# Two pre-norm layers on one core: first output weights two heads later, buffers of their own for x, and other places for layer 1's scale chain and bias quarters

## The chip, the cores and the metric

One core of a Trainium2 chip runs the kernel. The metric is the device time of one execution in microseconds (us). The times below are the median of three runs and one profiled execution. PE is TensorE (matmuls; PEld its weight loads), DVE VectorE, ACT ScalarE, POOL GpSimd, SP the engine whose queue issues the DMAs.

## The reference

Input x has 4 batches of 512 tokens with 1024 features, all float32. Two layers follow each other, each an attention and a feed-forward part with a residual addition and a layer norm in front:

```
x = x + L0_attn(ln(x))     # softmax over the 4 batches at each position
x = x + L0_ffn(ln(x), ...) # x @ W_base.T + b + LoRA of the top 2 of 8 experts
x = x + L1_attn(ln(x), ...)# 32 heads, causal, rope, low-rank q and kv; out @ wo.T
x = x + L1_ffn(ln(x), ...)
```

```
def _L1_ffn_ref(x, W, b, A, B, router_W, router_b):
    q = x[:, Q_START:Q_END, :].mean(axis=1)          # Q_START = 179, Q_END = -1
    routing = softmax(q @ router_W.T + router_b)     # 8 experts, one set per batch
    base = x @ W.T + b
    t = einsum('bsd,erd->bser', x, A)                # rank 16
    return base + einsum('bser,eor,be->bso', t, B, routing) * 2
```

## The kernel before

Tokens are cut into 16 tiles of 128. A float32 product is made as three matmuls of rounded parts: each operand is split into a high part h (rounded by a copy on ACT) and a low part l (the difference), and `matmul3` (L143 to L145) adds h*l, l*h and h*h in PSUM. Where both operands allow it, pairs of tiles and halves of the features make a 2 x 2 block product with seven products instead of eight; `STEPS` lists the seven (b11, t1, t2, b22, t3, b21, t4), with the PSUM bank and the quarter of the result of each. The operands of the seven steps are blocks and sums of blocks: s1, s2, s4, s3 (L934 on DVE), each split into h (ACT, L942: `ah`, `cxh`) and l (POOL, L943: `al`, `cxl`).

**Attention of layer 1** (about 430 to 1500 us of the profile) works on 4 groups of 8 heads, each on 4 batches. A loop over all heads u interleaves by hand the scores of head u (`pss`, with the mask and the row extremum on DVE in L868 and the exponential on ACT in L871), the transposes and values of the head before, the context of the pair before that, and, as a filler, either the output projection of the block before (`project`) or, in the first batch of a group, `prepare_output`. The latter multiplies slices of wo and wv into the output weights of the group: `block` (L1016: four matmuls into the PSUM tile poa or pob, which are read out by ACT in L1025 and L1030), and further steps that form and split their sums. `per` says how many steps of the filler are taken at each of three places of a head; 22 are needed. For the first block `per` is (0, 1, 2). The slices come by `fetch_output` on SP (2 x 512 KB and 64 KB for each two blocks), the next ones when a second half block has been issued. In this stretch a scheduler orders each engine's instructions by expected times; `issue_after` ties an instruction behind another one in its engine's order.

**The passage.** The projection of the last block (L1307 to L1330) is written for itself, with T, V, A and G in program order from there to the end (`manual_schedule`); SP's queue alone is still ordered by the scheduler. `fetch_last(j)` loads four 128 x 512 quarters of x from the scratch copy x_d into tiles xs of the pool xsp (order (0,0), (1,1), (0,1), (1,0)); each of the seven steps adds a product on DVE (L1328), and a finished quarter is stored (L1330). After the first add come the five small instructions of `scales` (L1245 to L1252) for the layer norm's scale and offset, and the next operand (s, cxh, cxl). Then load the weights of the last part, the bias row broadcast to all partitions (bias1, 512 KB), and rwT, rb, t3, t4.

**Layer 1's feed-forward** (about 1540 to 1776 us) runs over q = 0 to 7, each a pair of tiles, with seven steps of two products (columns 0 to 575 and 576 to 1151 of A and W together, 288 wide). One product is 12 matmuls, 1.60 us. Beside them in each step: `pair_sums`, `operand` (splits the operand two steps ahead), the statistics of the next pair (bn_stats L1519, bn_aggr L1520 in steps 1 and 2), `root` (ACT, L1238, step 2), `scales` (step 3), `norm` (ACT, L1260, steps 3 and 4), `turn1` (transposes L1269, steps 4 and 5). The product's results are added to x in place (`product`, L1458; its first 128 columns of LoRA inputs to `inputs`, L1454 and L1456). The LoRA of pair q - 1 follows within q: `weighed` multiplies inputs by the routing weights (hw, L1419), transposes (L1423), splits (hwh on ACT L1426, hwl on DVE L1428), and `lora` multiplies by B (lo, L143 to L145) and adds (L1412). For odd q this is at steps 2 to 5, for even q at steps 0 to 2; the routing weights rw are made by `mixture` (L1378 to L1400) at the turn from even to odd q.

`biased(q, n)` (POOL, L1436) adds one quarter of the bias row to a quarter of a tile of x, 128 x 256, in place: n = 0 to 3 for the first tile, 4 to 7 for the second. Before, pair q has two quarters at each of steps 1 to 4; those of q = 0 are at steps 0 to 3 of q = 1. They are issued behind the step's `operand` and ahead of its products:

```
            if q and 1 <= step < 5:
                for n in (0, 1):
                    biased(q, 2 * step - 2 + n)
            if q == 1 and step < 4:
                for n in (0, 1):
                    biased(0, 2 * step + n)
            if q:
                product(q, step, 0, h, l)
```

Of the kernel before, what the change touches and what calls it, by code (L numbers as in the profile page):

```python
# [9 lines left out]
F32 = mybir.dt.float32  # L10
# [7 lines left out]
P = 128  # L18
# [28 lines left out]
def block_kernel(ctx: ExitStack, tc: tile.TileContext, a: dict, out: bass.AP):  # L47
# [753 lines left out]
    with ExitStack() as c2:  # L801
# [17 lines left out]

        turn_of = [None]  # L820

        turned_in = [rdp.tile([P, 32], F32, name=f"ri{k}") for k in range(2)]
        for t in turned_in:
            G.memset(t, 0.0)
# [22 lines left out]
        def scores(u):  # L847

            g, b, i_ = units[u]
            f, h, l = queries.pop(u)  # L850
            _, kT, kF, _ = batches[g, b]
            p = pp.tile([P, 1280], F32, name="p")
            mn = small.tile([P, TPB], F32, name="mn")
            if i_ % 2 == 0:
                sums_of[0] = small.tile([P, 2, TPB], F32, name="rs2")
            rs2 = sums_of[0]
            rs = rs2[:, i_ % 2, :]
            for i in range(TPB - 1, -1, -1):
                n = (i + 1) * P
                ps = pss.tile([P, S], F32, name="pss")  # L860
                if i == 0:
                    T.matmul(ps[:, 0:n], lhsT=f[:, 0:P], rhs=kF, start=True, stop=True)
                else:
                    at = slice((i - 1) * P, i * P)
                    matmul3(ps[:, 0:n], h[:, at], l[:, at], kT[:, 0, 0:n], kT[:, 1, 0:n],
                            start=True, stop=True)
                to = p[:, OF[i] : OF[i] + n]
                turn_of[0] = V.tensor_tensor_reduce(out=to, in0=ps[:, 0:n], in1=causal[:, S - n : S], scale=1.0,  # L868
                                                    scalar=-NEG, op0=ALU.add, op1=ALU.min,
                                                    accum_out=mn[:, i : i + 1])  # L870
                A.activation(to, to, AF.Exp, bias=mn[:, i : i + 1], scale=-1.0,  # L871
                             accum_out=rs[:, i : i + 1])
                if i > 0:
                    yield
            if i_ % 2:
                divisors(u, rs2)
            probs[u] = p
            yield
# [122 lines left out]
        def prepare_output(g, fetched):  # L1001
# [9 lines left out]
            def block(n, half, at):  # L1011
                nonlocal fetched
                wo, wv = fetched
                po[at] = pso.tile([P, 512], F32, name="po" + at)
                for k in range(2):
                    T.matmul(po[at][k * KVR : (k + 1) * KVR, :], lhsT=wv[:, k, :],  # L1016
                             rhs=wo[k][:, half * 512 : half * 512 + 512], start=True, stop=True)
                if half and n + 1 < len(prs):
                    fetched = fetch_output(g, prs[n + 1])

# [135 lines left out]
        for u in range(NU + 3):  # L1156


            B, i = divmod(u - 3, HG)
            g, b = divmod(B, NB)  # L1160
            if i == 0 and B > 0:
                filler = project(*divmod(B - 1, NB))
            per = ((4, 1, 0) if i % 2 else (1, 1, 0)) if b else (2, 2, 2) if i >= HG // 2 else (3, 3, 1)
            if B == 0:
                per = (0, 1, 2)
            if b == 0 and i == (HG // 2 if g else 0) and g < NG:
                filler = prepare_output(g, wo_raw)
            sc = scores(u) if u < NU else iter(())
            tn = turn(u - 1) if 0 < u <= NU else iter(())
            if u >= 3 and u % 2:  # L1170
                cx = context(u - 3)
            advance(sc)
            advance(sc)
            advance(cx)
            advance(filler, per[0])
            if u + 1 < NU:
                split_query(u + 1)
            advance(sc)
            advance(sc)
            advance(tn)  # L1180
            advance(tn)
            advance(filler, per[1])
            if u < NU:
                g, b, i = units[u]
                if (b, i) == (NB - 1, 3) and g + 1 < NG:
                    wqs[2 * g + 2] = prepare_query(wq_raw, pso, "pob")
                if (b, i) == (0, 0) and g > 0:
                    wqs[2 * g + 1] = prepare_query(wq_raw, pso, "pob")
            if u + 2 < NU:
                query(u + 2, psq, "psq")  # L1190
            if u + 2 < NU:
                rotate_query(u + 2)
            advance(filler, per[2])
            advance(tn)
            if u < NU:
                g, b, i = units[u]
                if i == 2 and u + HG < NU:
                    nx = units[u + HG]
                    batches[nx[:2]] = load_batch(*nx[:2])
                if b == 0 and i == 0:  # L1200
                    wo_raw = fetch_output(g, 0)
                if (b, i) in ((NB - 1, 0), (NB - 1, 4)) and g + 1 < NG:
                    wq_raw = fetch_query(2 * g + 2 + i // 4)
                if (g, b) == (NG - 1, NB - 1) and i == 1:
                    late = raw()
                    hs = {0: [late[:, (t + 1) * D : (t + 2) * D] for t in range(2)]}
                    load_x(0, hs[0])
                    nc.sync.dma_start(out=late[:, 0:D], in_=a["b1T"])
                if (g, b) == (NG - 1, NB - 1) and i in (4, 5):
                    load_w1("t" + "12"[i - 4], 0, (0, 2)[i - 4])  # L1210
# [8 lines left out]
        w1p += [dp.enter_context(tc.tile_pool(name="d_w0", bufs=1))]  # L1219
        abp = dp.enter_context(tc.tile_pool(name="d_a", bufs=1))  # L1220
        splits = dp.enter_context(tc.tile_pool(name="d_split", bufs=3))
        ptp = dp.enter_context(tc.tile_pool(name="d_pt", bufs=2, space=PSUM))
        NP = NT // 2
        blocks, sums, roots, offs = {}, {}, {}, {}
# [78 lines left out]
        def fetch_last(j):  # L1303
            for t, k in ((0, 0), (1, 1), (0, 1), (1, 0)):
                at[j + t, k] = x_d[(NB - 1) * TPB + j + t][k]
                xs[j + t, k] = xsp.tile([P, 512], F32, name="xs")
                nc.sync.dma_start(out=xs[j + t, k], in_=at[j + t, k])  # L1307

        fetch_last(0)
# [4 lines left out]
        for n in range(14):  # L1314
# [36 lines left out]
                pair_sums(n - 10)  # L1351
            if n in (11, 12):
                parts.append(next(ops))
    w1p += [dp.enter_context(tc.tile_pool(name="d_w1", bufs=1, side="right"))]
    hp = dp.enter_context(tc.tile_pool(name="d_h", bufs=1))
    w1r = dp.enter_context(tc.tile_pool(name="d_c", bufs=1, side="right"))
# [5 lines left out]
        load_w1(kind, 1)  # L1362
    load_w1("t2", 1)
    fetch_h(1)
    bias1 = broadcast_rows(w1r, a["b1"], D, "bias1")
    rwT = w1r.tile([P, E, ND], F32, name="rwT")
    nc.sync.dma_start(out=rwT, in_=a["rwT"])
    rb = broadcast_rows(w1r, a["rb"], E, "rb")
    for kind in ("t3", "t4"):
        load_w1(kind, 1)  # L1370
    ones = w1r.tile([P, P], F32, name="ones")
    V.memset(ones, 1.0)
    bt1 = [w1r.tile([P, D], FR, name=f"b1{k}") for k in "hl"]
# [102 lines left out]
            split_w1("b22", 1, (step - 5,), V)  # L1476
    mix, at_work = None, {}

    def go_on(*keys):
        for k in keys:  # L1480
            next(at_work[k])

    for q in range(NP):
# [4 lines left out]
        for step in range(7):  # L1488

            if step == 6 and more:  # L1490
                pair_sums(0)
            if q and step < 2:
                for k in ((1, 2), (3,))[step]:
                    pair_sums(k)
# [5 lines left out]
            if odd and step in (1, 2):  # L1500
                rw[q // 2] = next(mix)
            if odd and step == 2:
                for t in range(2):
                    at_work[q - 1, t] = weighed(q - 1, t)
                    go_on((q - 1, t))
            if behind and step == 0:
                for t in range(2):
                    at_work[q - 1, t] = weighed(q - 1, t)
                    go_on((q - 1, t))
# [3 lines left out]
            if more and q + 1 >= TPB // 2:  # L1513
                if step == 1:
                    mv = small.tile([P, 2, 2], F32, name="mvd")
                if step in (1, 2):
                    st = small.tile([P, 2, 6], F32, name="st")
                    for c in range(2):
                        V.bn_stats(st[:, c, :], hs[q + 1][step - 1][:, c * 512 : (c + 1) * 512])  # L1519
                    V.bn_aggr(mv[:, step - 1, :], st)  # L1520
                if step == 2:
                    mv, r = root(mv, 2)
                if step == 3:
                    scales(mv, r, 2, range(2 * q + 2, 2 * q + 4))
            if more and step in (3, 4):
                norm(q + 1, step - 3)
            if q and 1 <= step < 5:
                for n in (0, 1):
                    biased(q, 2 * step - 2 + n)
            if q == 1 and step < 4:  # L1530
                for n in (0, 1):
                    biased(0, 2 * step + n)
            if q:
                product(q, step, 0, h, l)

            if (odd and step == 4) or (behind and step == 1):
                go_on((q - 1, 0), (q - 1, 1))
# [117 lines left out]
```

## Time and profile before

| | |
|---|---|
| runs of the kernel | 1781.0, 1783.48, 1784.86 us; median 1783.48 us |
| profiled execution | 1777.1 us, of which span 1775.3 us; around it 1.8 us |
| mean granted TensorE clock | 0.995 |
| ACT: exponentials of the scores (L871) | 512 x 559 ns = 284.5 us |
| POOL: splits `cxl` and others of 128 x 256 (L943) | 128 x 765 ns = 96.9 us |
| POOL: bias quarters (L1436) | 64, median 0.735 us each |
| DMA | 228.16 MB, mean 129 GB/s |

Times within the profile are microseconds from the span's start. The profiled execution stands at 6.4 us below the median of the runs, so differences are formed against its own time and then put on the median. In the timeline a row has start, length, engine, line, operation, what it writes and reads, and in brackets how long the engine had idled and what ended it. Matmuls are pipelined: rows of PE overlap.

### The profile page before, as it was taken

How to read it: one execution, taken by the hardware profiler on the slowest of the kernel's cores; microseconds unless marked ns; L12 is line 12 of the kernel's file. 1: busy time of each engine (PE TensorE's matmuls, PEld its weight loads, DVE VectorE, ACT ScalarE, POOL GpSimd, SP SyncE). 2: the span in 40 equal slices, each digit the busy share in tenths (PEclk: the TensorE clock that was granted, in tenths of full speed). 3: DMA queues.
4: the chain of work that ended last, by engine and by line, in shares of the span. 5: the costliest groups of instructions: out<-in, count | busy, mean ns of one | idle time of the engine just before them, and what ended most of it. 6: DMA issues, size and time to landing. Idle time of an engine off the chain costs nothing.

```text
span 1775.3 us, 31519 instructions
## 1 busy us (share of the span) xinstructions
PE 1724.4 (97%) x10536; PEld 1437.0 (81%) x10536; DVE 1315.3 (74%) x3516; ACT 904.0 (51%) x2319; POOL 884.3 (50%) x851
## 2 busy tenths in 40 slices
PE   6989999999999999999999999999999999999999
PEld 5989999998667778757777767778776877789998
DVE  6977885676787777687777787677778777587685
ACT  7422331365665555475555475555566555453332
POOL 0543441201556565546566545666555655575454
PEclk9999999999999999999999999999999999999999
DMA  4312454245133334352343353242354323944431
GB/s 191 120 51 92 165 172 130 84 137 184 57 123 129 98 106 136 108 180 87 120 132 101 115 188 108 93 148 93 127 164 135 118 100 114 328 159 136 140 111 61
DMA packets 131939, 228.16 MB, mean 129 GB/s; under 512 B 22272, under 2 KB 58752, under 8 KB 128448
## 3 DMA queue, kind: packets, MB, share of 16 engines
q1 hardware_dynamic: 131776, 226.13, 38.4%
q8 instruction: 84, 1.38, 0.3%
q14 instruction: 79, 0.65, 0.1%
HBM read 156.60 MB, written 71.83 MB: 129 GB/s over the span
## 4 chain that ended last, share of the span: by engine, by line
PE 85%; DVE 7%; DMA 3%; ACT 2%; issue 1%; POOL 1%; SPq 0%; DVEq 0%; POOLq 0%; ACTq 0%
PE psv L908 9%; PE pst L892 7%; PE pss L143 4%; PE pss L144 4%; PE pss L145 4%; PE po L143 4%; PE po L145 3%; PE po L144 3%; PE poa L143 3%; PE pob L143 3%; PE psq L143 3%; PE psq L145 3%; PE psq L144 3%; PE poa L144 3%; PE poa L145 3%; PE pob L145 3%
## 5 line engine op out<-in xcount | busy, mean ns | idle before, releaser
L871 ACT ACTIVATE p<-p,mn 128x512 f32<-128x512 f32 (+3 forms) x512 | 284.5, 559 | 206.0 <-DVE mn L868 205.8
L691 POOL TENSOR_TENSOR qf<-qf,ropeT 64x512 f32<-64x512 f32 x128 | 165.3, 1291 | 276.4 <-ACT qf L687 275.3
L868 DVE CUSTOM_DVE_ANT_0 p<-pss,causal 128x512 f32<-128x512 f32 (+3 forms) x512 | 231.2, 486 | 32.8 <-PE pss L145 25.5
L692 POOL TENSOR_TENSOR qf<-qf,t 64x512 f32<-64x512 f32 x128 | 165.7, 1294 | 41.0 <-DVE t L690 32.7
L892 PE MATMUL pst<-ident,p 128*128 128x128 f32 x1280 | 185.3, 273 | 0.7 <-ACT pT L894 0.7
L892 PEld LDWEIGHTS pst<-ident,p 128*128 128x128 f32 x1280 | 152.9, 141 | 25.6 <-ACT pT L894 2.4
L894 ACT COPY pT<-pst 128x512 f32<-128x512 f32 x256 | 141.7, 580 | 47.5 <-PE pst L892 46.7
L700 POOL TENSOR_TENSOR ql<-qf,qh 128x384 fp32r<-128x384 f32 x128 | 129.7, 1013 | 66.7 <-DVE qh L699 66.7
L143 PE MATMUL pss<-kT,ql 128*128 128x512 f32 (+2 forms) x384 | 144.6, 377 | 4.1 <-POOL ql L700 1.5
L943 POOL TENSOR_TENSOR cxl<-s,cxh 128x256 fp32r<-128x256 f32 x128 | 96.9, 765 | 89.5 <-ACT cxh L942 61.2
L143 PE MATMUL po<-w_h,hTl 128*128 128x384 f32 (+1 forms) x384 | 134.2, 350 | 0.6 <-DVE x L394 0.6
L145 PE MATMUL po<-w_h,hTh 128*128 128x384 f32 (+1 forms) x384 | 131.0, 341 | 0.0
L144 PE MATMUL pss<-kT,qh 128*128 128x512 f32 (+2 forms) x384 | 130.8, 341 | 0.0
L144 PE MATMUL po<-w_l,hTh 128*128 128x384 f32 (+1 forms) x384 | 130.7, 340 | 0.0
L145 PE MATMUL pss<-kT,qh 128*128 128x512 f32 (+2 forms) x384 | 130.3, 339 | 0.0
L894 DVE COPY pT<-pst 128x256 f32<-128x256 f32 x128 | 54.0, 422 | 96.3 <-PE pst L892 95.9
L687 ACT COPY qf<-psq 128x512 f32<-128x512 f32 x126 | 73.9, 587 | 70.3 <-PE psq L145 69.7
L689 DVE TENSOR_TENSOR t<-psq,ropeT 32x512 f32<-32x512 f32 x126 | 87.7, 696 | 23.9 <-ACT qf L687 19.9
L143 PEld LDWEIGHTS pss<-kT,ql 128*128 128x128 f32 x384 | 72.6, 189 | 39.3 <-POOL ql L700 11.2
L871 ACT ACTIVATION_READ_ACCUMULATOR p<-p,mn 128x1 f32 x512 | 97.4, 190 | 0.0
L690 DVE TENSOR_TENSOR t<-psq,ropeT 32x512 f32<-32x512 f32 x126 | 87.1, 691 | 1.8
L985 DVE TENSOR_TENSOR xs<-xs,pob 128x512 f32<-128x512 f32 x105 | 71.2, 678 | 19.6 <-PE pob L145 19.5
(563 smaller groups left out, 4977.6 us busy)
## 6 DMA issues: line engine op xcount, KB each, us to landing
xs<-x_d SPq DMA_DIRECT2D x128, 256.0 KB
x_d<-xs SPq DMA_DIRECT2D x128, 256.0 KB
slotC<-in_woT_dram SPq DMA_DIRECT2D x32, 512.0 KB
rb<-r_d SPq DMA_DIRECT2D x128, 128.0 KB
w_t<-raw SPq DMA_DIRECT2D x32, 288.0 KB
x<-in_x_dram SPq DMA_DIRECT2D x16, 512.0 KB
x_d<-x SPq DMA_DIRECT2D x32, 256.0 KB
slotA<-q_d SPq DMA_DIRECT2D x8, 1024.0 KB
```

The costliest lines, as they stand in the source:

```text
L143: T.matmul(ps, lhsT=al, rhs=bh, start=start, stop=False, **kw)
L144: T.matmul(ps, lhsT=ah, rhs=bl, start=False, stop=False, **kw)
L145: T.matmul(ps, lhsT=ah, rhs=bh, start=False, stop=stop, **kw)
L691: G.tensor_tensor(f[mid], f[mid], ropeT[mid, 0, :], ALU.mult)
L692: G.tensor_tensor(f[mid], f[mid], t2[mid], ALU.add)
L700: G.tensor_tensor(l, f[:, P:S], f32(h), ALU.subtract)
L868: turn_of[0] = V.tensor_tensor_reduce(out=to, in0=ps[:, 0:n], in1=causal[:, S - n : S], scale=1.0, scalar=-NEG, op0=ALU.add, op1=ALU.min, ...
L871: A.activation(to, to, AF.Exp, bias=mn[:, i : i + 1], scale=-1.0, accum_out=rs[:, i : i + 1])
L892: T.transpose(ps[:, w : w + P], p[:, OF[i] + j * P : OF[i] + (j + 1) * P], ident)
L894: copy(pT[:, AT[js[0]] : AT[js[0]] + w], ps[:, 0:w])
L908: T.matmul(ps[n * KVR : (n + 1) * KVR, S - w : S], lhsT=k[:, j, :], rhs=pTs[u + n][:, AT[j] : AT[j] + w], start=(j == 0), stop=(j == TPB - 1))
L943: G.tensor_tensor(l, src, f32(h), ALU.subtract)
```

## The change

Six edits, line numbers of the kernel before:

1. `prepare_output`'s blocks are tied behind the last score matmul that has been issued (`scored[0]`), and `per` of the first block becomes (0, 0, 0) for its first two heads and (0, 2, 2) from the third on.
2. A pool d_xl of three buffers takes the quarters (0,0), (1,1) and (0,1) that `fetch_last(0)` loads; (1,0) and the four of `fetch_last(2)` stay in xsp. The pool is closed after the projection.
3. The load of bias1 is issued behind those of t3 and t4.
4. `scales` moves from the head of step 3 to step 2, behind that step's first product.
5. For even q the two hw of `weighed` go ahead of `pair_sums` in step 0.
6. The bias quarters move: q = 0 to steps 0, 1 and 3 of q = 1 (three, three and two), even q to steps 3 to 6, odd q to steps 4 to 6 and step 0 of q + 1, q = 7 to steps 1, 3, 4 and 5.

```diff
                 if i == 0:
-                    T.matmul(ps[:, 0:n], lhsT=f[:, 0:P], rhs=kF, start=True, stop=True)
+                    scored[0] = T.matmul(ps[:, 0:n], lhsT=f[:, 0:P], rhs=kF, start=True, stop=True)
...
-                for k in range(2):
-                    T.matmul(po[at][k * KVR : (k + 1) * KVR, :], lhsT=wv[:, k, :],
-                             rhs=wo[k][:, half * 512 : half * 512 + 512], start=True, stop=True)
+                with tc.issue_after(scored[0].ins):
+                    for k in range(2):
+                        T.matmul(po[at][k * KVR : (k + 1) * KVR, :], lhsT=wv[:, k, :],
+                                 rhs=wo[k][:, half * 512 : half * 512 + 512], start=True, stop=True)
...
             if B == 0:
-                per = (0, 1, 2)
+                per = (0, 2, 2) if i > 1 else (0, 0, 0)
...
+        xl = ExitStack()
+        xlp = xl.enter_context(tc.tile_pool(name="d_xl", bufs=3))
...
-                xs[j + t, k] = xsp.tile([P, 512], F32, name="xs")
+                xs[j + t, k] = (xsp if j or (t, k) == (1, 0) else xlp).tile([P, 512], F32, name="xs")
...
+        xl.close()
...
-    bias1 = broadcast_rows(w1r, a["b1"], D, "bias1")
     rwT = w1r.tile([P, E, ND], F32, name="rwT")
     nc.sync.dma_start(out=rwT, in_=a["rwT"])
     rb = broadcast_rows(w1r, a["rb"], E, "rb")
     for kind in ("t3", "t4"):
         load_w1(kind, 1)
+    bias1 = broadcast_rows(w1r, a["b1"], D, "bias1")
...
+    BIASED = {(q, step): [] for q in range(NP) for step in range(7)}
+    for q in range(NP):
+        places = ([(1, 0), (1, 1), (1, 3)] if q == 0 else
+                  [(q, 3), (q, 4), (q, 5), (q, 6)] if q % 2 == 0 else
+                  [(q, 4), (q, 5), (q, 6), (q + 1, 0)] if q + 1 < NP else
+                  [(q, 1), (q, 3), (q, 4), (q, 5)])
+        for n in range(8):
+            BIASED[places[n * len(places) // 8]].append((q, n))
...
+            if behind and step == 0:
+                for t in range(2):
+                    at_work[q - 1, t] = weighed(q - 1, t)
+                    go_on((q - 1, t))
             if q and step < 2:
                 for k in ((1, 2), (3,))[step]:
                     pair_sums(k)
...
-            if behind and step == 0:
-                for t in range(2):
-                    at_work[q - 1, t] = weighed(q - 1, t)
-                    go_on((q - 1, t))
...
-                if step == 3:
-                    scales(mv, r, 2, range(2 * q + 2, 2 * q + 4))
...
-            if q and 1 <= step < 5:
-                for n in (0, 1):
-                    biased(q, 2 * step - 2 + n)
-            if q == 1 and step < 4:
-                for n in (0, 1):
-                    biased(0, 2 * step + n)
+            for p, k in BIASED[q, step]:
+                biased(p, k)
             if q:
                 product(q, step, 0, h, l)
+            if more and q + 1 >= TPB // 2 and step == 2:
+                scales(mv, r, 2, range(2 * q + 2, 2 * q + 4))
```

More of the change, by code (lines that the diff above doesn't have):

```diff
@@ L820, in block_kernel @@
         turn_of = [None]
+        scored = [None]
         turned_in = [rdp.tile([P, 32], F32, name=f"ri{k}") for k in range(2)]
```

## The prediction

> **What bounds the kernel now.** I read the shares of the page first, then PE's waits over the span, then the timeline around each wait that the change touches, then windows for the clock.
>
> ```profile
> PE 1724.4 (97%) x10536; PEld 1437.0 (81%) x10536; DVE 1315.3 (74%) x3516; ACT 904.0 (51%) x2319; POOL 884.3 (50%) x851
> PE 85%; DVE 7%; DMA 3%; ACT 2%; issue 1%; POOL 1%; SPq 0%; DVEq 0%; POOLq 0%; ACTq 0%
> ```
>
> PE is the bound. The change takes no matmul away, and the compiled order of PE's instructions differs only inside the first attention block (rows of 430 to 545 us). So it can win or lose only where PE waits, and PE's waits that it can reach are few:
>
> ```profile
> PE lo L143 <- DVE hwl L1428: 5.8, 4, 2.7
> PE poa L1016 <- issue: 2.1, 1, 2.1
> PE acc L143 <- issue: 1.9, 1, 1.9
> PE pob L143 <- POOL cxl L943: 1.4, 3, 1.1
> ```
>
> (Total us, times, longest.) The first is layer 1's, the second the first output weights', the last two the passage into layer 1. Under 12 us are to be had in all; what decides is which new waits the change sets.
>
> **First output weights (430 to 545 us).** Before, PE ends a score tile at 434.1, waits 2.1 us for kT, runs the eight block matmuls (L1016) from 436.25 to 439.3, and takes the third score tile up at 440.22, when DVE's first L868 (439.46 to 440.15) has freed the PSUM tile. That L868 also waits for the landing of the kT_d store that SP issued at 436.18, since its tile lies on old memory. After, the two blocks leave this hole, but the hole stays: kT_d sets it, and at best L868 starts some 0.7 us sooner. The blocks come back two heads later in a stretch where PE is full; there two of their matmuls take 1.07 us (rows at 463.42 and 465.29), so the two blocks that moved cost 4 x 0.53 = 2.1 us. Back comes 0.4 us (the exp table load of ACT, 1.28 us at 439.98, no longer stands behind the copies L1025 and L1030). The 512 KB fetches that follow on SP move later with the blocks; nothing waits for them but L1016, whose DMA wait is 0.5 us in the whole span, so I put them at 0 (0.5 at most). Bounds: +0.5 (kT_d lands early) to +2.5; I take +1.3.
>
> **The buffers of x (1515 to 1560 us).** The new pool takes three tiles, the tile (1,0) stays in xsp. In the compiled order SP's early free slot (issued at 1502.9 before) goes to (1,0), needed late, while (0,0), needed first, is queued on SP behind the four stores of the block before it, the last issued at 1519.74:
>
> ```profile
> 1520.16 1.94 SPq L1307 DMA_DIRECT2D xs<-x_d  x4
> ...
> 1520.19 0.69 DVE L1328 TENSOR_TENSOR xs<-xs,poa 128x512 f32<-128x512 f32 x1 [0.48 <-PE poa L145]
> ...
> 1523.03 0.69 DVE L1328 TENSOR_TENSOR xs<-xs,pob 128x512 f32<-128x512 f32 x1 [0.46 <-PE poa L145]
> ...
> 1523.95 0.51 PE L143 MATMUL pob<-b220h,cxl 128*128 128x512 f32 x1 [1.06 <-POOL cxl L943]
> ```
>
> The DVE add at 1523.03 had to wait for a load issued at 1520.16: 2.8 us. In the changed kernel the add of 1520.19 waits for a load issued at that same moment, so it starts at about 1523.0. Behind it on DVE stand the five scale instructions and s (L934), then cxh on ACT, cxl on POOL, and PE's b220: 3.07 us from the add's end (1520.88) to 1523.95. The add ends at 1523.7; with DVE's small gaps closed, PE starts b220 at about 1526.4 instead of 1523.95: +2.4 us (2.0 to 2.8), and PE has then idled 1.1 + 2.4 = 3.5 us.
>
> Then the clock. After the 1.9 us wait of `acc` at 1547 the granted clock falls (columns: window, length, busy us of PE, PEld, DVE, ACT, POOL, then PEclk, DMA share, GB/s):
>
> ```profile
> 1548.00:1552.00 4.00, 2.89 (x14) 2.92 (x15) 1.03 (x5) 0.61 (x3) 1.26 (x1) 0.71 1.03 425
> 1552.00:1556.00 4.00, 4.00 (x28) 4.00 (x28) 4.00 (x8) 2.45 (x6) 2.42 (x2) 0.87 1.00 407
> ```
>
> Twelve matmuls there start 240 ns apart instead of 133: 1.3 us, and 1.6 with the rest of the spell. The 1.1 us wait at 1523.95 left the clock at 1.00. The Trainium skill ("TensorE: Matmul & The Clock Gate", Part 1: The HAM clock gate) says that the clock halves after an idle window of about 3.4 us and returns after as long a busy one. By that rule the 1.9 us wait should have cost no clock, and 3.5 us of idleness should; by the row 1.9 us suffices. Both make the new wait at 1526 cost a spell, +1.5 us (0 if the window falls badly); they differ on the old one: by the rule nothing is to be won there beyond 1.9 us, by the row up to 3.5. I go by the row.
>
> That old wait: DVE's L1454 (to 1548.49) waits until the last store of x, issued at 1543.26, has landed, with the DMA engines at a share of 0.95 to 1.04 since 1536. After, three 256 KB loads lie ahead of this stretch instead of in it (0.77 MB; the windows from 1536 to 1548 move 335 to 407 GB/s, so some 2.1 us of queue), but the stores still follow PE. I take 0.7 of the 1.9 us wait and half of the spell, together -1.5 (0 to -3.5), and -0.8 for SP no longer standing behind a store at 1534.5. The passage: +2.4 + 1.5 - 2.3 = +1.6 (-1.5 to +4). The later bias1 load (512 KB) is used first at about 1577 and is hidden.
>
> **Layer 1, what is won (1566 to 1776 us).** PE's products take 1.60 us each; odd q lose time at step 4:
>
> ```profile
> 1643.29 1.29 POOL L943 TENSOR_TENSOR al<-a,ah 128x512 fp32r<-128x512 f32 x1 [2.51 <-ACT ah L942]
> ...
> 1643.42 1.17 DVE L1248 SCALAR_TENSOR_TENSOR nt<-mvd,nt 128x2 f32<-128x2 f32 x1
> ...
> 1644.54 1.43 POOL L1436 TENSOR_TENSOR xo<-xo,bias 128x256 f32<-128x256 f32 x2
> ...
> 1644.63 0.67 DVE L1250 SCALAR_TENSOR_TENSOR y2d<-nt,y 128x2 f32<-128x2 f32 x1
> ...
> 1645.34 0.65 DVE L1252 SCALAR_TENSOR_TENSOR off<-mvd,y2d 128x2 f32<-128x2 f32 x1
> ...
> 1647.45 0.49 DVE L1428 TENSOR_TENSOR hwl<-pt,hwh 128x128 fp32r<-128x128 f32 x2 [0.23 <-ACT hwh L1426]
> ...
> 1647.79 0.50 PE L143 MATMUL lo<-b1h,hwl 128*128 128x512 f32 x1 [1.14 <-DVE hwl L1428]
> ```
>
> A 128x2 operation that takes 0.16 us alone ends with POOL's operation. The two hw of step 2 last 1.53 us beside the quarters, against 0.49 at 1605. With the chain a step sooner and the quarters out of steps 1 to 3, about 1.0 (hw) + 0.9 (y2d, off) + 0.2 leave DVE's way to hwl. PE waits 1.14 us in q = 3 and 5, so all of it would go, but DVE enters these q 1 us later (next part): -1.0 each. In q = 1 the wait is 2.7 us and DVE also waited 1.44 us for a quarter of q = 0 (1586.83): -3.0 with the 0.3 of the transposes. Won: 5.0 (4 to 6.5).
>
> **Layer 1, what is added.** Each quarter stands in POOL's order behind the al of the same step. At odd q, step 6, the DVE add of product (6,0) needs a quarter that is now there:
>
> ```profile
> 1601.69 0.45 DVE L1458 TENSOR_TENSOR xo<-xo,acc 128x288 f32<-128x288 f32 x1
> ...
> 1602.56 1.29 POOL L943 TENSOR_TENSOR al<-s,ah 128x512 fp32r<-128x512 f32 x1 [5.54 <-ACT ah L942]
> ...
> 1603.17 0.45 DVE L1458 TENSOR_TENSOR xo<-xo,acc 128x288 f32<-128x288 f32 x1 [1.03 <-PE acc L145]
> ```
>
> al ends at 1603.85, two quarters of 0.74 us follow, so that add starts at 1605.3 instead of 1601.69. Behind it on DVE: the second add, both hw, two s, two adds of raw. hw, which PE transposes at 1606.16, comes at 1606.7: +0.5. Of the 3.5 us, DVE's idle 1.03 and 0.47 absorb 1.5; hwl (1609.63 before, when PE took it at once) comes 2.0 later, against a PE that is 0.5 later: +1.5. Three times (q = 1, 3, 5): 3 x 2.0 = +6.0. At even q, step 6, the add of (6,1) needs a quarter behind the al of 1630.02: al ends 1631.32, plus 0.74 is 1632.05 instead of 1630.31; `each` comes at 1634.0 where PE wants it at 1633.3: 3 x 0.6 = +1.8 (q = 2, 4, 6). The tail (q = 7) moves two quarters one step; DVE has 1 us of idleness there: 0 (up to +0.7). Bounds: +2 if the slack is larger than I count, +9 if it is smaller; I take +7.8. Layer 1: +7.8 - 5.0 = +2.8.
>
> **Sum.** 1.3 + 1.6 + 2.8 = +5.7 us: the profiled 1777.1 would become 1782.8. That execution was 6.4 us quicker than the median of 1783.48; on the median the forecast is 1789.2, say 1789. A measurement of this kernel can tell about 0.2% (3.6 us) from no change.
>
> **Rivals.** (a) Full price: nothing comes back at 1547 (passage +3.9), the quarters cost +9, the blocks +2.1, the gain is 4: +11, 1794.5. For it: DMA stays at a share near 1 whatever is loaded first. Against: 0.77 MB less in that stretch. (b) Not slower: the one mechanism is POOL's quarter ahead of the add at step 6. If POOL reaches it before the add is due (it would have to be done by 1603.2, 2.1 us sooner than I work out, so that DVE's 1.5 us of idleness covers the rest) the 7.8 falls to about 0.5 and odd q win 5.8: 1.3 + 1.6 - 5.3 = -2.4, 1781. For it: POOL was idle 5.54 us before that al. Against: the order on POOL puts al first, and al waits for ACT. (c) The passage turns: the last store lands before PE asks, wait and spell go (-3.5), and the spell at 1526 doesn't come: 2.4 - 4.3 = -1.9 for the passage, +2.2 in all, 1785.5. (d) The tie doesn't bite: PE's order shows that the blocks do move, so only the place counts, and I leave it inside the forecast.
>
> **Chances.** Forecast (1786 to 1792) 0.47, (a) 0.18, (b) 0.22, (c) 0.13. Of the forecast 0.03 is within 0.2%; (b) splits 0.15 faster, 0.07 same; (c) 0.04 faster, 0.07 same, 0.02 slower. Faster 0.19, same 0.17, slower 0.64. Range: from inside (b) to beyond (a), 1778 to 1797.
>
> **What would show it.** Right: the DVE xo add of odd q's step 6 names POOL as its releaser with 3 to 3.5 us; PE's lo waits sit in even q instead of odd; L1328's first add waits about 2.8 us for a DMA and b220 comes 3.5 us late; L1016 stands between score tiles of later heads. Wrong: no such POOL waits, or half clock gone from 1549, which would take the sum below +2.

## The result and the profile after

The changed kernel takes 1789.23 us (median of six runs, 1788.05 to 1792.46), the kernel before 1782.24 us (six runs, 1779.04 to 1785.24): ratio 1.0041, 95% interval 1.0025 to 1.0057, so slower by 4.5 to 10.2 us, about 7. The forecast was 1789, or +5.7 on the median of 1783.48 us that the first three runs of before had.

The page of the changed kernel (span 1788.8 us, execution 1790.6 us):

```profile
PE 1726.5 (97%) x10536; PEld 1436.8 (80%) x10536; DVE 1307.3 (73%) x3516; ACT 904.9 (51%) x2319; POOL 886.2 (50%) x851
PE 8%; DVE 3%; issue 1%; DMA 1%; POOL 1%; ACT 0%; SPq 0%; DVEq 0%; ACTq 0%; POOLq 0%
```

The work is the same. The shares of the chain (second line) add up to 14% of the span: it was followed back through the last part only, and is of no use for the whole. PE's waits over the span (total, times, longest):

```profile
PE lo L143 <- DVE hwl L1434: 7.0, 5, 1.7
PE pss L143 <- DVE mn L870: 7.0, 2, 6.8
...
PE poa L143 <- DVE y L1250: 2.4, 1, 2.4
...
PE acc L143 <- POOL al L945: 1.4, 2, 1.3
PE acc L143 <- DVE wb L1150: 1.2, 1, 1.2
...
PE pob L143 <- DVE xs L1333: 1.0, 1, 1.0
...
PE acc L143 <- issue: 0.5, 1, 0.5
```

The lo waits have grown from 5.8 to 7.0 us and changed sides (below); the 2.1 us ahead of the blocks has become 6.8 us ahead of the third score tile; the 1.9 us wait at 1547 has shrunk to 0.5, and four others stand around it (2.4 at poa, 1.0 at pob, 1.3 for al, 1.2 for wb), in the place of one of 1.1.

**How profiles are compared here.** PE's order is the same in all kernels outside 430 to 545 us, so the start of one and the same matmul can be compared between two traces. I cut the span at 428, 548, 1515 and 1568 us of the first profile. One execution differs from the next by some us even where the code is the same: the profile after is 13.4 us longer than the first profile of before, of which 2.5 us come before 428 us. The stretches of all kernels, as differences from the first profile of before (us), with the ratio of the runs:

| kernel | 428-548 | 1515-1568 | 1568-end | runs against before, 95% |
|---|---|---|---|---|
| changed kernel | +2.3 | +1.6 | +6.9 | 1.0041 (1.0025 to 1.0057) |
| e1: edit 1 | +1.0 | +1.7 | +1.4 | 1.0016 (1.0008 to 1.0023) |
| e2: edits 2, 3 | -1.0 | +3.3 | 0.0 | 1.0006 (0.9997 to 1.0015) |
| e3: edits 4, 5, 6 | +0.4 | +1.9 | +5.3 | 1.0023 (1.0014 to 1.0032) |
| e4: all, quarters ahead of al | +1.4 | +1.9 | +0.2 | 1.0018 (1.0010 to 1.0027) |
| e5: before again | +1.4 | +1.8 | 0.0 | one run, 1781.56 us |
| e6: edits 4, 5 | -1.3 | +3.3 | -1.3 | one run, 1778.04 us |
| e7: edit 6 | -0.8 | +1.9 | +5.1 | one run, 1782.94 us |
| e8: 4, 5, quarters ahead, other places | -0.5 | +2.4 | -3.2 | 0.9975 (0.9968 to 0.9983) |
| e9: edit 1, tie alone | +0.5 | +2.0 | +1.4 | 0.9999 (0.9989 to 1.0009) |
| e10: edit 1, later steps alone | -1.6 | +0.6 | +1.6 | 0.9990 (0.9982 to 0.9999) |
| e11: e8 with edits 2, 3 | -0.3 | +1.1 | -3.2 | 0.9976 (0.9967 to 0.9985) |
| e12: e8 with e10's half | -2.2 | +1.2 | -3.2 | 0.9966 (0.9954 to 0.9978) |

### The profile page after: what moved, and what is told of

It is laid out like the page before. It is cut to its first block, busy times and chain, and to the rows that moved or that the text cites. A ratio compares the mean times of both kernels' runs of the same rounds, so it can differ in the third digit from the quotient of the medians.

```text
span 1788.8 us, 31535 instructions
## 1 busy us (share of the span) xinstructions
PE 1726.5 (97%) x10536; PEld 1436.8 (80%) x10536; DVE 1307.3 (73%) x3516; ACT 904.9 (51%) x2319; POOL 886.2 (50%) x851
## 5 line engine op out<-in xcount | busy, mean ns | idle before, releaser
L873 ACT ACTIVATION_READ_ACCUMULATOR p<-p,mn 128x1 f32 x512 | 97.4, 190 | 0.0
```

## The experiments

**e1, edit 1 alone, and its two halves: e9 has the first line, e10 the last pair.**

```diff
+                with tc.issue_after(scored[0].ins):
                     for k in range(2):
...
-                per = (0, 1, 2)
+                per = (0, 2, 2) if i > 1 else (0, 0, 0)
```

> Only edit 1 (output weights two heads later and tied) on the kernel before. My theory: the hole that the two blocks leave is not filled, because the first mask row of DVE (L868 before) waits for the kT_d store; PE idles about 7 us there instead of 2.1 + 0.9 us, and the two blocks cost their 2.1 us again two heads later: +2 us (1.5 to 2.5) in that stretch, and in all. Rival: the tie is free, because PE finds the 2 us in idle places of the later heads: 0 (-0.5 to 0.5).

> Half of edit 1: the blocks tied behind the last score matmul, but the steps begun at head 0 as before (0, 1, 2). In PE's order the first two blocks then leave the hole ahead of the third score tile. If leaving the hole is what edit 1 costs, the stretch from 428 to 548 us is 1.5 to 2 us above the mean of the kernels without edit 1 (-0.3 us against the first profile), and PE idles about 7 us in front of the third score tile. If the later steps are the cost, 0 (-0.5 to 0.5).

> The other half of edit 1: (0, 0, 0) and (0, 2, 2) without the tie. In PE's order the first two blocks then stay in the hole, only the later ones move by two heads. If leaving the hole is the cost, 0 (-0.5 to 0.5) against before; if the later steps are, 1.5 to 2 us more.

e1 is 2.8 us slower (1.4 to 4.1). The hole is as expected; this is the timeline of the changed kernel (start, length, engine, line, what is written from what, and what ended the idle time):

```profile
438.72 0.58 SPq L770 DMA_DIRECT2D kT_d<-kT  x1
439.35 1.80 SPq L972 DMA_DIRECT2D xs<-x_d  x3
...
442.74 0.69 DVE L870 CUSTOM_DVE_ANT_0 p<-pss,causal 128x512 f32<-128x512 f32 x1 [4.05 <-DMA kT_d<-kT]
```

DVE's first mask row waits for the kT_d store, with the blocks in the hole or without (the first profile of before named PE's blocks there, e5 names the store). It starts 4.0 us after the store's issue here and in e9, 3.1 us in e1 and e4, and 2.8 to 3.9 us in the ten profiles where the blocks stay in the hole: no difference beside the scatter, though three 256 KB loads now follow the store at once on SP and one before. Nothing is won from the hole, and PE idles 6 to 7 us in e1, e4, e9 and the changed kernel.

In the stretch, the three kernels with the whole of edit 1 stand at +1.0, +1.4, +2.3 (mean 1.6), the eight without any of it, the first profile among them, at -0.3 on the mean (-1.3 to +1.4): +1.8 us. The halves don't add up to it. The tie alone makes the same hole, yet costs 0.8 us in its one profile and nothing in the runs (within 2 us); the later steps alone leave the blocks in the hole and gain 1.8 us (0.2 to 3.2). So the hole is not a price of 2 us by itself.

Where the price falls shows when the stretch is cut once more behind the hole, at one and the same transpose (452.12 us in the first profile) where the clock is at 1.00 in all kernels. From there to the end of the stretch, before and in the changed kernel (window, length, busy us of PE, PEld, DVE, ACT, POOL, then PEclk, DMA share, GB/s):

```profile
452.12:548.02 95.90, 94.57 (x510) 66.31 (x510) 75.61 (x206) 64.33 (x173) 52.71 (x49) 1.00 0.29 94
455.47:552.84 97.37, 95.68 (x519) 66.16 (x518) 75.17 (x206) 66.52 (x176) 52.79 (x49) 1.00 0.33 104
```

The three kernels with the whole of edit 1 take 97.4 us, e9 95.6, e10 and e12 95.1, and those without edit 1 95.8 to 96.1 (e5 97.0, with one wait of 1.5 us for a load of slotC). The waits are nearly alike, 1.7 us against 1.3 to 1.6 (but for e5); it is PE's own work that grows from at most 94.6 to 95.7 us, and shrinks to 93.9 in e9 and 93.5 in e10. Most of the difference lies in the matmuls marked 128*64, those of the blocks and of the values (psv): 25.0 us without edit 1, 23.6 in e10 and e12, and with the eight more that the tie brings here 25.9 in the three, 25.3 in e9. How they stand in PE's order decides their time. A block that the order tears in two, in the first profile (two rows), and a whole one in the changed kernel:

```profile
463.42 1.07 PE L1016 MATMUL poa<-slotC 128*64 128x512 f32 x2
...
465.29 1.07 PE L1016 MATMUL poa<-slotC 128*64 128x512 f32 x2
```

```profile
475.28 1.08 PE L1019 MATMUL poa<-slotC 128*64 128x512 f32 x4
```

Four matmuls take the time of two. So what edit 1 costs depends on how the new order joins or tears these matmuls. That is read from the traces; no run changes the joining alone, and the rest of the difference, 1 us in e9, is open.

**e2, the buffers and the bias row alone, and e5, the kernel before again.**

```diff
-                xs[j + t, k] = xsp.tile([P, 512], F32, name="xs")
+                xs[j + t, k] = (xsp if j or (t, k) == (1, 0) else xlp).tile([P, 512], F32, name="xs")
...
+        xl.close()
...
     fetch_h(1)
-    bias1 = broadcast_rows(w1r, a["b1"], D, "bias1")
...
     for kind in ("t3", "t4"):
         load_w1(kind, 1)
+    bias1 = broadcast_rows(w1r, a["b1"], D, "bias1")
```

> Only edits 2 and 3 (pool d_xl, bias1 load later). My theory: (0,0) is loaded behind the four stores, so the first add L1328 waits about 3 us and PE loses 2.5 us at 1521; the 1.9 us wait at 1547 and its spell at half clock (together 2.9 us) go, but the weight splits L1147 on DVE, which were hidden beside that spell, then make PE wait 2 us: +1.7 us (0 to 3) in all. Rival: the splits' wait comes from elsewhere (layer 1's edits), then the passage alone is 0 or a gain of 0.3 us.

> The kernel before, profiled once more. If the passage into layer 1 varies by itself (the single-edit kernels without d_xl also showed the early stall and none of the 1.9 us wait), this profile shows the DVE add of xs waiting over 1 us longer at 1523 and the wait at 1547 shorter, 1.5 to 2 us more between 1515 and 1567 than the first profile. If edit 2 alone is behind the passage's loss, the passage is as in the first profile (within 0.5 us).

The new first wait is as forecast. Timeline of the changed kernel:

```profile
1525.24 3.21 SPq L1312 DMA_DIRECT2D xs<-x_d  x7
...
1528.10 0.69 DVE L1333 TENSOR_TENSOR xs<-xs,poa 128x512 f32<-128x512 f32 x1 [3.36 <-issue]
...
1528.93 0.47 PE L143 MATMUL poa<-t20h,cxl 128*128 128x512 f32 x1 [2.40 <-DVE y L1250]
```

The load of (0,0) is issued at 1525.24, the add that needs it starts 2.9 us later after 3.4 us of idleness (the row names no releaser; that it is the load is read from the order), and PE waits 2.4 us (3.7 in e2) at t20, which writes the poa that the add reads. Still edit 2 costs little in the end. e1, e3 and others, which don't have it, show the passage 1.7 to 3.3 us above the first profile as well, and so does the unchanged kernel, e5. PE's waits of e5 between 1515 and 1570:

```profile
PE acc L143 <- DMA wt<-w_t: 2.3, 1, 2.3
PE acc L143 <- POOL al L943: 1.9, 2, 1.3
```

The first profile of before had the wait at 1547 and half clock behind it, and none of these; in e5 that wait is 0.6 us, the one at 1523 is 1.1 us as in the first profile, and PE waits for the load of the weights w_t instead, with half clock behind it (0.57 from 1568 to 1572). In the changed kernel the one at poa is there, and at the matmul of the w_t wait PE waits 1.2 us, by the view for DVE's splits wb and no longer for the load; e2 has 3.7 us at poa and 1.1 us left at w_t. Four kernels with edit 2 stand at 2.0 us on the mean in this stretch, ten without at 1.7 (0 to 3.3): no difference beside the scatter, and e11 below adds no time to e8. The rival's number for e2 (0) failed too: the passage varies by 3 us on its own. The DMA engines are near a share of 1 here for some 40 us (0.91 to 1.07 in e5's windows from 1522 to 1562), and PE waits somewhere in it: in sum 6.2 to 7.0 us in the four profiles with edit 2 and 5.4 to 7.2 in nine without. Only the first profile has less, 3.6 us, and half clock with it. So a wait set ahead is made up for by less at later places. That the transfers are what keeps the sum is likely, not shown: in the changed kernel the DMA share is 0.68 from 1544 to 1554, and its last wait is put down to DVE.

**e3, layer 1's edits alone; e6 and e7, its two parts:** e6 has the move of `scales` (and edit 5), e7 that of the quarters, with the places of the change.

```diff
-                if step == 3:
-                    scales(mv, r, 2, range(2 * q + 2, 2 * q + 4))
...
             if q:
                 product(q, step, 0, h, l)
+            if more and q + 1 >= TPB // 2 and step == 2:
+                scales(mv, r, 2, range(2 * q + 2, 2 * q + 4))
...
-            if q and 1 <= step < 5:
-                for n in (0, 1):
-                    biased(q, 2 * step - 2 + n)
...
+            for p, k in BIASED[q, step]:
+                biased(p, k)
```

> Only edits 4, 5 and 6 (scales a step sooner, hw ahead, bias quarters elsewhere). My theory: the whole of layer 1's loss is here: lo waits of odd q shrink by 4.4 us, DVE adds of odd q's step 6 wait 3.5 us for POOL and cost PE 2.3 us three times, even q's step 6 cost 0.5 us three times, the tail 1.3 us, and up to one spell at half clock of 1.6 us: +5 to +7 us. Rival: half of that loss came from the later arrival at layer 1 or from the bias1 load: then +2.8 us as forecast, or less.

> Only edits 4 and 5 (scales a step sooner, hw ahead of the sums at even q), quarters as before. If the scales' step is what wins at odd q, the lo waits of q = 3 and 5 shrink from 1.14 us to under 0.3 and layer 1 is 2 to 4 us below before; if the quarters' leaving steps 1 to 3 is what wins, under 1 us. If hw ahead of the sums costs at even q, PE waits up to 1 us there.

> Only edit 6 (the quarters' places). My theory: the DVE adds of odd q's step 6 wait 3.5 us for POOL and the stalls at even q (2.3 us each), at the turn (0.5 us each) and in the tail (1.3 us) are all here: layer 1 is +6 to +9 us against before, as the gain of the scales is missing. Rival: without hw ahead of the sums the stall at even q is under 1 us each, +1 to +3 us.

e3 has most of the loss: +5.3 us in the stretch, 4.1 us by the runs (2.5 to 5.7). The added wait, in the timeline of the changed kernel:

```profile
1607.11 1.29 POOL L945 TENSOR_TENSOR al<-s,ah 128x512 fp32r<-128x512 f32 x1 [4.13 <-issue]
1608.36 1.43 POOL L1442 TENSOR_TENSOR xo<-xo,bias 128x256 f32<-128x256 f32 x2
...
1609.82 0.82 DVE L1464 TENSOR_TENSOR xo<-xo,acc 128x288 f32<-128x288 f32 x2 [3.49 <-POOL xo L1442]
...
1616.42 0.53 PE L143 MATMUL lo<-b1h,hwl 128*128 128x512 f32 x1 [1.74 <-DVE hwl L1434]
```

al, two quarters, and only then the add: DVE stands for 3.49 us (3.5 forecast), hwl is late, PE waits 1.74 us at lo. And what was won, in q = 3:

```profile
1648.23 0.49 DVE L1425 TENSOR_TENSOR hw<-inputs,rw 128x128 f32<-128x128 f32 x2
...
1651.12 1.27 DVE L1255 SCALAR_TENSOR_TENSOR y2d<-nt,y 128x2 f32<-128x2 f32 x1
1652.43 0.16 DVE L1257 SCALAR_TENSOR_TENSOR off<-mvd,y2d 128x2 f32<-128x2 f32 x1
...
1654.56 0.48 DVE L1434 TENSOR_TENSOR hwl<-pt,hwh 128x128 fp32r<-128x128 f32 x2
...
1655.52 0.39 PE L143 MATMUL lo<-b1h,hwl 128*128 128x512 f32 x1
```

hw is back at 0.49 us and off at 0.16, while y2d still takes 1.27 us beside al (POOL, 1651.08 to 1652.37); lo no longer waits. Which of the edits did that, the two parts tell. In e6 (scales a step sooner, quarters as before), q = 3:

```profile
1641.17 1.52 DVE L1419 TENSOR_TENSOR hw<-inputs,rw 128x128 f32<-128x128 f32 x2
...
1646.40 0.66 DVE L1252 SCALAR_TENSOR_TENSOR off<-mvd,y2d 128x2 f32<-128x2 f32 x1
```

In e7 (quarters moved, scales as before):

```profile
1641.10 0.50 DVE L1419 TENSOR_TENSOR hw<-inputs,rw 128x128 f32<-128x128 f32 x2
...
1645.48 0.16 DVE L1252 SCALAR_TENSOR_TENSOR off<-mvd,y2d 128x2 f32<-128x2 f32 x1
```

It is the quarters' leaving. At odd q, e7 wins 1.5, 1.4 and 1.4 us (q = 1, 3, 5), e6 only 0.5 each: less than it expected if the step were the cause, more than nothing. e7 pays 2.1 us at each even q, 0.6 at each turn and 1.3 in the tail, in all +5.1, less than the 6 to 9 expected because the gain at odd q is here and not with the scales. The rival there (under 1 us at even q without hw ahead of the sums) is out.

**e4, the quarters ahead of al; e8, other places as well; e11 and e12 on top of it.**

```diff
+            for p, k in BIASED[q, step]:
+                biased(p, k)
             if step == 6 and more:
                 pair_sums(0)
...
             h, l = operand()
...
+        places = ([(1, 0), (1, 1), (1, 2), (1, 3)] if q == 0 else
+                  [(q, 3), (q, 4), (q, 5), (q, 6)] if q % 2 == 0 else
+                  [(q, 4), (q, 5), (q, 6)] if q + 1 < NP else
+                  [(q, 1), (q, 2), (q, 3), (q, 4)])
```

e4 is the changed kernel with the first of these (the quarters ahead of the sums and of `operand`) and its own places; e8 has edits 4 and 5 on the kernel before, with both; e11 adds edits 2 and 3 to e8, e12 the later, untied half of edit 1.

> The changed kernel with one difference: each step's quarters are issued ahead of that step's pair_sums and operand, so that on POOL they stand ahead of al and not behind it. If the place behind al is the cause, the DVE adds no longer wait for POOL at step 6, and PE gets back 7 us (odd to even), 1.7 us (even to odd), 1.3 us (tail) and the spell: 6 to 11 us below the changed kernel, 1 us above to 3 us below the kernel before. Rival (the loss is that hw stands ahead of the sums, or that POOL has too much work in steps 5 to 0): no more than 2 us below the changed kernel.

> The kernel before with edits 4 and 5, and with the quarters ahead of each step's al: q = 0 as before in steps 0 to 3 of q = 1, even q in steps 3 to 6, odd q in steps 4 to 6 and none beside the hw of the next q, q = 7 in steps 1 to 4. If the place behind al and the quarters beside hw and s are the whole of the loss, no lo wait of over 0.4 us is left but in q = 1 and layer 1 is 3 to 5 us below before, 0.2% in all. Rival: what is left in the kernel with the quarters ahead (1.2 us at each even q) comes from hw ahead of the sums: then layer 1 is 0 to 1 us below before.

> The best kernel so far (quarters ahead of al, odd q in steps 4 to 6) with edits 2 and 3 added. If the passage is bound by the landing of the weights w_t, edit 2 only moves PE's wait from there to the first add: a wait of 2.4 to 3.7 us at poa behind the scales, none or 1.1 us left at the wt load, and the whole within 1 us of the kernel without it. If edit 2 has a price of its own: 1.5 to 2.5 us slower than that kernel.

> The version that the runs point to: edits 4 and 5, the quarters ahead of al with odd q in steps 4 to 6, and the later, untied half of edit 1; edits 2 and 3 and the tie left out. If the two gains add (4.5 us of the quarters, 1.8 us of the later blocks): 5 to 7 us below before. If the gain of the later blocks was scatter of the measurement: 4 to 5 us, as without them. Layer 1 is 3 us below the first profile either way.

e4 stands at +0.2 us in layer 1, 6.7 us below the changed kernel and 5.1 below e3: the place behind al is the cause of most of the loss. By the runs it is about 4 us below the changed kernel (1.0018 against 1.0041), less than the 6 to 11 expected, since 1.2 us stay at each even q and most of q = 1's gain is gone. The timeline of e4 shows the former, at the turn from q = 1 to 2:

```profile
1608.88 0.45 DVE L1464 TENSOR_TENSOR xo<-xo,acc 128x288 f32<-128x288 f32 x1
...
1610.72 1.21 DVE L1425 TENSOR_TENSOR hw<-inputs,rw 128x128 f32<-128x128 f32 x2
1611.00 1.53 POOL L1442 TENSOR_TENSOR xo<-xo,bias 128x256 f32<-128x256 f32 x2
1611.86 1.22 DVE L936 TENSOR_TENSOR s<-s,a 128x512 f32<-128x512 f32 x1
```

The add no longer waits, but hw and s run beside the two quarters of step 0 and take 1.21 and 1.22 us instead of 0.49 and 0.86. e8 takes these quarters away: layer 1 is at -3.2 us, and nothing is added at even q, the turns and the tail. The longest of PE's waits in it:

```profile
PE acc L143 <- DVE y L1245: 1.0, 1, 1.0
PE acc L143 <- DVE xo L1458: 1.0, 1, 1.0
PE lo L143 <- DVE hwl L1428: 0.7, 1, 0.7
```

The wait at lo is that of q = 7, at the very end, which the kernel before has too (0.75 us). The two at acc are in q = 1, where the quarters of q = 0 still run: lo no longer waits there, but PE waits at two products instead, and q = 1 wins 0.6 us against 1.3 and 1.4 in q = 3 and 5.

e8 is 4.5 us faster than before (3.0 to 5.7). The rival, that hw ahead of the sums is what is left, is out: e8 has it too. e11 is at the same ratio, so edits 2 and 3 add nothing. e12, at 1774.76 us, is 6.1 us faster than before (3.9 to 8.2), the best of all; the two gains seem to add, though the step from e8 to e12 is within the intervals.

## Why the prediction was right, step by step

**The sum** (+5.7 against about +7) and the main mechanism, DVE's add behind POOL's al and quarters, are right; the parts less so. With means over all profiles of each code: first weights +1.8 (1.6 less -0.3), passage +0.3, layer 1 +5.4 (6.1 from e3 and the changed kernel, less 0.7 from the six profiles with layer 1 as before: 0, 0.0, 0.0, 1.4, 1.4, 1.6). Together 7.5. Layer 1 was nearly twice as dear as forecast (+2.8), and most of the +1.6 of the passage was not there; that these two errors cancel in part is luck. So is how near 1789.23 lies to the 1789 forecast, since the median of before came down by 1.2 us with three more runs.

- **First output weights**, +1.3 forecast, +1.8 in the profiles, +2.8 by the runs of e1. The hole stays, as forecast, and 1.5 us are lost behind it. The 2.1 us for the two blocks is a right figure from a wrong working: two blocks are eight matmuls, and at the 0.53 us each of the two rows used they would cost 4.3 us; they cost about 2 because a block that is not torn takes 1.08 us in the changed kernel. Nor is it a fixed price: e9 moves the same eight matmuls behind the hole, and PE's work there is 0.6 us less than before.
- **Buffers of x**, +1.6 forecast. Right: the load that decides, the 2.4 us at PE (2.4 measured, though at t20, with 1.0 us left at b220, where the forecast had 3.5 in one), the old wait at 1547 shrinking. Wrong: the spell at half clock behind the new wait. The changed kernel's granted clock stays at 1.00 from 1524 to 1536, though PE waits 2.4 and 1.0 us shortly after each other. The old spell is gone as well (1.00 from 1548 to 1564). That was named as a sign of being wrong that would take the sum below +2, and both turns of rival (c) came but for 0.5 us of the wait, yet the passage is not shorter: PE waits 1.3 and 1.2 us at two later places. So a fixed price and a partial relief were the wrong terms: with edit 2 and without it PE's waits here come to about the same sum, at other places. That the profile after shows +1.6 here is an accident, since the unchanged kernel shows +1.8 in its second profile. The forecast took one execution's passage for the kernel's. It also read the old wait as one for the last store of x; the row of the first profile names a load of the weights wb instead, and no run tells the two apart:

```profile
1548.49 0.29 DVE L1454 COPY inputs<-acc 128x128 f32<-128x128 f32 x1 [3.89 <-DMA wb<-w_b]
```

- **Layer 1, won**: 5.0 forecast, 4.8 measured, in the changed kernel as in e3: 2.0 (q = 1), 1.4 and 1.4. The forecast had 3.0, 1.0 and 1.0, so the errors cancel. In q = 1 PE waits 1.0 us at a product (acc, for DVE's xo) where it did not before; the quarters of q = 0 still run there, three in a step, and that they are the reason is likely and wasn't tested alone. The chain's step, named first in the change, brings 0.5 of about 1.4 us when made alone.
- **Layer 1, added**: 2.0 each at even q forecast, 2.4 in e3; 0.6 each at the turns, 0.6 measured. The tail was put at 0 (up to 0.7) and costs 1.3 us: a DVE add waits 1.76 us for the quarters of step 4 behind POOL's last al, hwl stands behind that add, and PE's lo behind hwl. The idleness counted there does not lie ahead of this add. In all about 10 us against 7.8. In the changed kernel one more price falls due: at q = 2 the lo wait of 1.74 us is followed by half clock. Its window (busy us of PE, PEld, DVE, ACT, POOL, then PEclk, DMA share, GB/s):

```profile
1617.00:1621.00 4.00, 4.00 (x17) 3.52 (x17) 2.56 (x4) 0.00 (x0) 1.09 (x1) 0.60 0.24 92
```

It costs 1.6 us, is absent in e3 with the same waits, and appears in three of the six profiles with q = 1's old wait of 2.7 us. Those three are e1, e9 and e10, which have edit 1 or a half of it; whether that is chance is not shown.

Of the rivals, (b) named the right mechanism for what would turn the sign: once the quarter is not behind al, and not beside hw, layer 1 is 3.2 us below before.

## What to carry to other kernels

An operation moved to an engine with spare time is due not when that engine is idle but when its order lets it come: put it ahead of the instruction there that waits for others, or the consumer pays for both. Count also what it slows on another engine by running beside it: two quarters of POOL beside DVE's hw and s cost 1.2 us at each even q, half of what they had cost behind al. Before a filler is moved on PE, see whether the new order joins or tears matmuls that go faster together. And where the DMA engines are near a share of 1, judge an edit by more than one profile of the unchanged kernel: at the passage a wait moved from place to place with the sum nearly kept.

## What was not expected of the hardware

- Half clock followed the 1.74 us wait of q = 2 in the changed kernel and not in e3, where the code of layer 1 is the same; it followed the 2.7 us wait of q = 1 in three profiles of six; and waits of 2.4 and 1.0 us close together left the clock at 1.00. The Trainium skill ("TensorE: Matmul & The Clock Gate", Part 1: The HAM clock gate) has the window of about 3.4 us run freely, which fits the dependence on where a wait falls, but not the figure as a least idle time.
- An operation of DVE on 128x2 numbers takes 0.16 us alone and 1.27 us beside al of POOL, and then ends with it (y2d above, at 1652.39, al at 1652.37). TENSOR_SCALAR rw, 128x8, took 0.23 us in e7 and 1.26 us in e6 and before.
- The same store of kT_d was waited for until 2.8 to 4.0 us after its issue, from one profile to the next.
- Four block matmuls of 128*64 took 1.08 us together, and two of them 1.07 us where the order had torn them apart.
